# Two LoRA layers in one kernel: features dealt out anew, both weights loaded 32 partitions at a time, and a second product of the weights in seven parts

## The chip, the cores and the metric

The kernel runs on one core of a Trainium2 chip. The core has a matrix engine (TensorE, PE in the profile), three engines for elementwise work (VectorE or DVE, ScalarE or ACT, GpSimd or POOL), a sequencer that does nothing here but issue transfers (SyncE or SP), and 16 DMA engines that carry the transfers. PE reads SBUF and writes PSUM, which has eight banks of 128 x 512 float32. The metric is the device time in microseconds, the median of several runs; lower is better. All data are float32.

## The reference, cut to what matters

```python
# L0: labeler_index has 8 entries here; x is (8, 256, 1024)
base  = einsum('bsi,oi->bso', x, W0)
low   = einsum('bsi,bir->bsr', x, lora_A0[labeler_index])      # rank 32
x = x + base + einsum('bsr,or->bso', low, lora_B0_w) * 0.5
# L1
base  = einsum('bti,oi->bto', x, W1) + b
low   = einsum('bti,bir->btr', x, lora_As1[adapter_mapping])   # rank 16
x = x + base + einsum('btr,bro->bto', low, lora_Bs1[adapter_mapping]) * 2.0
```

W0 and W1 are 1024 x 1024; x has 2048 rows. With the residuals a layer is x(I + W^T) plus a term of low rank. The kernel multiplies the two layers together first, M = (I + W0)^T (I + W1)^T, and then has one large product x M, with the adapters of both layers put into a term of rank 48 and a bias row.

## The kernel before, in words

**M = A B by blocks.** A comes from W0 as loaded (`w0n`, 128 partitions x 8 chunks x 1024), B from W1 transposed (`w1T`, same shape). Both are cut in 2 x 2 blocks of 512. The outer scheme has seven block products instead of eight; P1 = A11 B11 is wanted by itself (`m22` holds it for later), and M11 = A11 B11 + A12 B21. The 512 features between the layers that belong to half i are chunks 4i to 4i+3 of `w0n` and `w1T`: feature 512 i + 4 p + m lies at partition p, chunk 4 i + m.

**The seven groups of products before the main loop**, in PE's order:
- 15 warm-up matmuls on the identity (L918).
- P1: for each of four tiles m of 128 rows and four chunks k, a 128x256 matmul on the first 256 columns (`first`, L949 to L964), then the same on the other 256 (L967 to L970). `keep_p1` has ACT copy each tile's bank to `m22`.
- A12 B21 (`product2`, L308): 16 matmuls of 128x512, added in PSUM on top of P1; ACT copies the sums to `m11`.
- `prepare_down(0)` (L698): 8 matmuls of 128x512, whose stationary operand is `a1`, the eight gathered adapter matrices of layer 1 side by side. It needs all eight.
- `prepare_up` (L668), `finish_up`, `prepare_down(1)`, `prepare_cross`, then the other block products of the weights (`w_groups`, `Chain`), of which the last are themselves split in seven by `product` (L514) with quarters of 128 x 256; `form` (L571) adds seven kept products up to four quarters on DVE.

**Loads.** SP issues everything that comes from DRAM for the weights: `load_w1` (four transfers of 32 partitions for each call, because DVE transposes W1 in blocks of 32 x 32, L225), `load_w0` (one transfer of 128 partitions for each chunk and half of the columns). `load_a1(b)` (L196) is different: ACT reads the index of batch b into a register (L197), issues one transfer of 64 KB from the chosen adapter (L198), and POOL copies it into `a1` (L202). It is called three batches at a time between the tiles of `product2` (L975).

**The identity.** I + W is made in place: a DVE or POOL instruction adds the identity on the diagonal of a chunk (L185 for `w0n`, L233 for `w1T`). DVE does those of the first half; POOL does those of the second half (L233 for h = 1, L982).

**The order.** The instructions of each of the five engines run in the order in which the program names them (`tc.manual_schedule(engines=ORDERED)`, L894). An instruction that waits holds everything behind it on its engine, transfers that the engine issues included. Waits between engines are put in by the compiler from the reads and writes of tiles.

Of the kernel before, what the change touches and what calls it, by code (L numbers as in the profile page):

```python
# [10 lines left out]
ALU = mybir.AluOpType  # L11
# [9 lines left out]
P = 128  # L21
NH = 512
# [5 lines left out]
NWARM = 15  # L28
NV7 = 7
# [5 lines left out]
NQ = NH // 2  # L35
NB = 4
NX = 2
SQ = 32
# [4 lines left out]
def kernel(  # L43
# [11 lines left out]
    lora_b1: bass.AP,  # L55
    out: bass.AP,
):

# [70 lines left out]
    def fix_indices(rawi, n: int, layer: int):  # L131
        wrap = const.tile([1, B], I32, tag=f"wrap{layer}", name=f"wrap{layer}")
        nc.vector.tensor_scalar(wrap, rawi, 0, n, ALU.is_lt, ALU.mult)
        fixed = const.tile([1, B], I32, tag=f"fixed{layer}", name=f"fixed{layer}")
        nc.vector.tensor_tensor(fixed, rawi, wrap, ALU.add)
        nc.vector.tensor_scalar(fixed, fixed, 0, n - 1, ALU.max, ALU.min)
        return fixed

    def index(fixed, b: int, n: int, engine=SP):
        return nc.values_load(  # L140
            fixed[0:1, b : b + 1],
            engines=[engine],
            min_val=0,
            max_val=n - 1,
            skip_runtime_bounds_check_because="clamped on the chip",
        )
# [11 lines left out]
                )  # L158
        return xq

    def new_w1(h: int, i: int):
        both = units[:, 4 * h + 2 * i : 4 * h + 2 * i + 2].rearrange("p u n -> p (u n)")
        return both.rearrange("p (t c) -> p t c", t=NR)

    def load_w1(wq, h: int, i: int, lo: int = 0, hi: int = NR):

        rows = slice(h * NH + lo * SQ, h * NH + hi * SQ)
        for g in range(NG):
            cols = slice(i * NH + g * P, i * NH + (g + 1) * P)
            nc.sync.dma_start(  # L170
                wq[g * SQ : (g + 1) * SQ, lo:hi, :],
                w1[rows, cols].rearrange("(t q) c -> q t c", q=SQ),
            )

    def load_w0(k: int, i: int):
        cols = slice(i * NH, (i + 1) * NH)
        rows = w0[(k // NB) * NH : (k // NB + 1) * NH, cols]
        nc.sync.dma_start(  # L178
            w0n[:, k, cols], rows.rearrange("(p m) c -> p m c", m=NB)[:, k % NB, :]
        )  # L180

    def diag_w0(k: int):
        diag = w0n[:, k].rearrange("p (i q m) -> p i m q", i=2, m=NB)[:, k // NB, k % NB]
        engine = nc.vector if k < NB else nc.gpsimd
        engine.tensor_tensor(diag, diag, ident, ALU.add)  # L185

    def load_b0():
        nc.sync.dma_start(
            b0.rearrange("p (i m) r -> p i (m r)", i=2),
            lora_b0.rearrange("(i p m) r -> p i (m r)", i=2, m=NB),  # L190
        )


    a1_rows = work[:, 0 : 2 * NH].rearrange("p (b k r) -> p b k r", b=B, k=NK)

    def load_a1(b: int):  # L196
        j = index(fixed1, b, N1, mybir.EngineType.Activation)  # L197
        nc.scalar.dma_start(  # L198
            a1_rows[:, b].rearrange("p (i m) r -> p i (m r)", m=NB),
            lora_a1[bass.ds(j, 1)].rearrange("o (i p m) r -> p (o i) (m r)", i=2, m=NB),  # L200
        )
        nc.gpsimd.tensor_copy(a1[:, :, b, :], a1_rows[:, b])  # L202

    def load_down(b: int):
# [15 lines left out]
            )  # L220


    def turn_w1(wq, h: int, k: int, lo: int = 0, hi: int = NR):
        cols = slice(h * NH + lo * SQ, h * NH + hi * SQ)
        nc.vector.transpose(  # L225
            w1T[:, k, cols].rearrange("p (t q) -> p t q", q=SQ),
            wq[:, lo:hi].rearrange("p t (q m) -> p m t q", m=NB)[:, k % NB],
        )
        if k // NB == h:
            part = slice(lo * SQ // NB, hi * SQ // NB)  # L230
            diag = w1T[part, k, cols].rearrange("p (q m) -> p m q", m=NB)[:, k % NB]
            engine = nc.vector if h == 0 else nc.gpsimd
            engine.tensor_tensor(diag, diag, ident[part, part], ALU.add)  # L233

    def turn_x(xq, unit: int):
        xT = units[:, unit].rearrange("p (k t) -> p k t", k=NB)
# [238 lines left out]
    def quarters(x):  # L475
        return x[:, 0:2, 0:P], x[:, 2:4, 0:P], x[:, 0:2, P:T], x[:, 2:4, P:T]

    def z_sums(x, z):
        x11, x12, x21, x22 = x
        nc.vector.tensor_tensor(z[0], x21, x22, ALU.add)  # L480
        nc.vector.tensor_tensor(z[1], z[0], x11, ALU.subtract)
        nc.vector.tensor_tensor(z[2], x11, x21, ALU.subtract)
        nc.vector.tensor_tensor(z[3], x12, z[1], ALU.subtract)


    SLOT = {2: 0, 3: 1, 4: 2, 5: 3, 7: 4, 1: 5, 6: 6}
# [3 lines left out]
    def slot(ps, i: int):  # L490
        n, pos = BANK[i]
        return ps[n][:, pos * NQ : (pos + 1) * NQ]
# [78 lines left out]
    def form(v, ps=None, dst=None):  # L571
# [21 lines left out]
        nc.vector.tensor_tensor(mid, src_two(3, 0), two(1), ALU.add)  # L593
        nc.vector.tensor_tensor(d[:, 3 * NQ : 4 * NQ], src(5), at(6), ALU.add)  # L594

    m12 = {}

    def sums_m(m: int):
# [5 lines left out]
    class Chain:  # L604
# [33 lines left out]
            z_sums(self.q(name), self.z[name])  # L638

        def preload(self):  # L640

            p = m22[:, self.tiles, :].rearrange("p m (h n) -> p (m h) n", h=2)
            for i, part in ((2, 0), (4, 2), (5, 3)):
                nc.scalar.copy(slot(self.X, i), p[:, part])
            nc.vector.tensor_tensor(slot(self.X, 3), p[:, 1], p[:, 3], ALU.subtract)
            for i in (1, 7):
                nc.vector.memset(slot(self.X, i), 0.0)

        def product(self, ps, name, which, first, low=None):
            product(ps, self.q(name), self.z[name], w_ops[which], first, low=low)  # L650
# [17 lines left out]
    def prepare_up():  # L668
        tile = work[:, 4 * NH : 6 * NH]
        part = [tile[:, h * NH : (h + 1) * NH] for h in range(NO)]  # L670
        for h in range(NO):
            cols = slice(h * NH, (h + 1) * NH)
            pm = new_bank()
            for k in range(NK):
                g = k % 4
                nc.tensor.matmul(  # L676
                    pm[g * R0 : (g + 1) * R0, :],
                    b0[:, k, :],
                    w1T[:, k, cols],
                    start=(k < 4),  # L680
                    stop=(k >= NK - 4),
                )
            nc.scalar.copy(part[h], pm)
        return part
# [13 lines left out]
    def prepare_down(h: int):  # L698
        pm = new_bank()
        for k in range(NK):  # L700
            nc.tensor.matmul(  # L701
                pm,
                a1[:, k].rearrange("p b r -> p (b r)"),
                w0n[:, k, h * NH : (h + 1) * NH],
                start=(k == 0),
                stop=(k == NK - 1),
            )
        nc.scalar.copy(gT[h], pm)
# [185 lines left out]
    with tc.manual_schedule(engines=ORDERED):  # L894
        make_identity(nc, ident)
        mid = NR // 2
        wq = {}
        wq[0, 0] = new_w1(0, 0)
        for n in range(2):
            load_w1(wq[0, 0], 0, 0, n * mid, (n + 1) * mid)  # L900
            if n == 0:
                for k in range(NB):
                    load_w0(k, 0)
        wq[0, 1] = new_w1(0, 1)
        load_w1(wq[0, 1], 0, 1)
        for k in range(NB, NK):
            load_w0(k, 0)
        for i in range(2):
            wq[1, i] = new_w1(1, i)
            load_w1(wq[1, i], 1, i)  # L910
        load_b0()
        for k in range(NK):
            load_w0(k, 1)
        nc.scalar.copy(s_all[:, 0:R0], ident[:, 0:R0])

        pw = banks[6][:, 0:P]
        for _ in range(NWARM):
            nc.tensor.matmul(pw, ident, ident, start=True, stop=True)  # L918
        raw0, raw1 = load_indices(idx0, 0), load_indices(idx1, 1)
        nc.gpsimd.memset(scale, L1_SCALING)  # L920
        for half in range(2):
# [27 lines left out]
        def first(g, k: int, n: int):  # L949
            cols = slice(n * NH // 2, (n + 1) * NH // 2)  # L950
            nc.tensor.matmul(  # L951
                g.p1[:, cols],
                g.a[0][:, k, :],
                w1T[:, k, cols],
                start=False,
                stop=(k == NB - 1),
                skip_group_check=True,
            )

        for k in range(NB):  # L960
            turn_w1(wq[0, 0], 0, k, 0, mid)
            diag_w0(k)
            for g in w_groups:
                first(g, k, 0)  # L964
        for k in range(NB):
            turn_w1(wq[0, 0], 0, k, mid, NR)
        for m, g in enumerate(w_groups):  # L967
            for k in range(NB):
                first(g, k, 1)
            g.keep_p1(m22[:, m, :])  # L970
        fixed0, fixed1 = fix_indices(raw0, N0, 0), fix_indices(raw1, N1, 1)
        for k in range(NB, NK):
            turn_w1(wq[0, 1], 0, k)
        for m, g in enumerate(w_groups):
            for b in range(3 * m, min(3 * m + 3, B)):  # L975
                load_a1(b)
            g.product2(m11[:, m, :])
        for k in range(NB):
            turn_w1(wq[1, 0], 1, k)
        for k in range(NB):  # L980
            turn_w1(wq[1, 1], 1, NB + k)
        for k in range(NB, NK):  # L982
            diag_w0(k)
        for k in range(NB):
            sums_w1_first(k)
        prepare_down(0)
        part = prepare_up()
        w_groups[0].sums()
        sums_w1_last()
        finish_up(part)  # L990
        prepare_down(1)
        prepare_cross()
        for which in ("t2", "t1"):
            w_ops[which].sums_dma()
# [286 lines left out]
```

## Time and profile before

| what | value |
|---|---|
| time, median of 3 runs (lowest, highest) | 336.07 us (335.89, 336.35) |
| time of the profiled execution | 336.54 us |
| its span, first to last instruction | 334.8 us |
| PE busy | 329.6 us, 1496 instructions |
| DVE busy | 246.2 us |
| ACT busy | 61.3 us |
| POOL busy | 67.9 us |
| P1's first matmul starts | 7.33 us |
| `product2` (16 matmuls of 128x512) | 22.32 to 36.05 us on the chain that ended last |

A span is the time from the first to the last instruction; the execution is 1.74 us longer than it. In the timeline a row has its start, its length (of several instructions, from the first start to the last end), the engine, the line, the operation, what it writes and reads, and in brackets how long the engine stood idle before it and what ended that. A float32 matmul is recorded as two instructions, so that x32 are 16 matmuls. PE's rows of weights being loaded (PEld) run beside its matmuls.

### The profile page before, as it was taken

How to read it: one execution, taken by the hardware profiler on the slowest of the kernel's cores; microseconds unless marked ns; L12 is line 12 of the kernel's file. 1: busy time of each engine (PE TensorE's matmuls, PEld its weight loads, DVE VectorE, ACT ScalarE, POOL GpSimd, SP SyncE). 2: the span in 40 equal slices, each digit the busy share in tenths (PEclk: the TensorE clock that was granted, in tenths of full speed). 3: DMA queues.
4: the chain of work that ended last, by engine and by line, in shares of the span. 5: the costliest groups of instructions: out<-in, count | busy, mean ns of one | idle time of the engine just before them, and what ended most of it. 6: DMA issues, size and time to landing. Idle time of an engine off the chain costs nothing.

```text
span 334.8 us, 4443 instructions
## 1 busy us (share of the span) xinstructions
PE 329.6 (98%) x1496; PEld 245.1 (73%) x1496; DVE 246.2 (74%) x466; ACT 61.3 (18%) x128; POOL 67.9 (20%) x125
## 2 busy tenths in 40 slices
PE   8999999999999999999999999999999999999996
PEld 8774434544488877888877887877888777788875
DVE  5752697159899999999997856985675986323964
ACT  1022043300034132440001330001331001322000
POOL 7001261540042232771023100012200010000000
PEclk9999999999999999999999999999999999999999
DMA  7949982990062980786277300275500121100113
GB/s 211 199 133 186 271 191 46 168 173 14 0 95 63 194 137 14 113 133 104 95 191 204 79 2 0 74 222 148 116 10 0 63 96 63 64 2 0 63 65 126
DMA packets 66399, 34.53 MB, mean 103 GB/s; under 512 B 47300, under 2 KB 61124, under 8 KB 66376
## 3 DMA queue, kind: packets, MB, share of 16 engines
q1 hardware_dynamic: 56520, 21.13, 27.9%
q0 software_dynamic: 7680, 12.59, 17.4%
q10 hardware_dynamic: 2176, 0.52, 1.0%
q8 instruction: 12, 0.20, 0.2%
q14 instruction: 11, 0.09, 0.1%
HBM read 19.55 MB, written 8.39 MB: 83 GB/s over the span
## 4 chain that ended last, share of the span: by engine, by line
PE 94%; DMA 2%; SPq 1%; DVE 1%; issue 0%; ACT 0%; DVEq 0%
PE bank L523 66%; PE bank L286 14%; PE bank L747 4%; PE bank L701 4%; DMA units<-in_L_cond_W_dram 2%; PE bank L951 2%; PE bank L676 1%; PE bank L765 1%; SPq L170 1%; DVE w1T L225 1%; PE bank L690 1%; SPq L178 1%; DVE w1T L233 0%; PE bank L736 0%; PE bank L715 0%
## 5 line engine op out<-in xcount | busy, mean ns | idle before, releaser
L509 DVE TENSOR_TENSOR work<-bank,work 128x512 f32<-128x512 f32 (+1 forms) x56 | 32.7, 620 | 19.0 <-PE bank L523 18.8
L505 ACT COPY work<-bank 128x512 f32<-128x512 f32 (+1 forms) x56 | 25.8, 548 | 43.0 <-PE bank L523 42.6
L225 DVE STREAM_TRANSPOSE w1T<-units 128x512 f32<-128x512 f32 (+1 forms) x20 | 17.3, 901 | 18.0 <-DMA units<-in_L_cond_W_dram 17.9
L888 POOL DMA_DIRECT2D out_dram<-work x12 | 9.0, 752 | 100.6 <-DVE work L594 100.6
L523 PE MATMUL bank<-w0n,w1T 128*128 128x256 f32 x104 | 24.6, 384 | 0.0
L755 ACT ACTIVATE a<-bank,shift,scale 128x256 f32<-128x256 f32 x8 | 4.5, 564 | 103.3 <-PE bank L747 103.3
L523 PEld LDWEIGHTS bank<-w0n,w1T 128*128 128x128 f32 x104 | 19.3, 190 | 4.1 <-issue 1.7
L523 PE MATMUL bank<-w0n,m 128*128 128x256 f32 x88 | 21.2, 384 | 0.0
L523 PE MATMUL bank<-w1T,s_all 128*128 128x256 f32 x80 | 20.2, 379 | 0.0
L238 DVE STREAM_TRANSPOSE units<-units 128x512 f32<-128x512 f32 x32 | 19.9, 676 | 0.2
L523 PEld LDWEIGHTS bank<-w0n,m 128*128 128x128 f32 x88 | 16.4, 190 | 3.4 <-issue 1.4
L523 PE MATMUL bank<-tw,m 128*128 128x256 f32 x68 | 17.5, 382 | 0.0
L523 PEld LDWEIGHTS bank<-w1T,s_all 128*128 128x128 f32 x80 | 15.2, 190 | 2.1
L523 PE MATMUL bank<-tw,s_all 128*128 128x256 f32 x64 | 16.1, 379 | 0.0
L747 PE MATMUL bank<-units,down 128*64 128x256 f32 x128 | 15.6, 385 | 0.0
L523 PE MATMUL bank<-m,units 128*128 128x256 f32 x64 | 15.1, 379 | 0.0
L951 PE MATMUL bank<-w1T,w0n 128*128 128x256 f32 x64 | 14.5, 383 | 0.5 <-DVE w1T L233 0.5
L523 PEld LDWEIGHTS bank<-tw,m 128*128 128x128 f32 x68 | 12.8, 190 | 2.4 <-issue 0.7
L523 PE MATMUL bank<-w0n,s_all 128*128 128x256 f32 x56 | 14.4, 379 | 0.0
L286 PE MATMUL bank<-tw,s_all 128*128 128x512 f32 x32 | 14.3, 595 | 0.0
L951 PEld LDWEIGHTS bank<-w1T,w0n 128*128 128x128 f32 x64 | 12.3, 196 | 2.4 <-DVE w1T L233 1.3
L701 PE MATMUL bank<-w0n,a 128*128 128x512 f32 x32 | 14.1, 592 | 0.0
(249 smaller groups left out, 646.8 us busy)
## 6 DMA issues: line engine op xcount, KB each, us to landing
units<-in_x_dram SPq DMA_DIRECT2D x128, 64.0 KB, 2.4
out_dram<-work POOLq DMA_DIRECT2D x12, 512.0 KB, 3.5
w0n<-in_L_cond_W_dram SPq DMA_DIRECT2D x16, 256.0 KB, 6.1
units<-in_L_cond_W_dram SPq DMA_DIRECT2D x12, 256.0 KB, 4.9
out_dram<-work SPq DMA_DIRECT2D x3, 512.0 KB, 3.2
units<-in_L_cond_W_dram SPq DMA_DIRECT2D x8, 128.0 KB, 4.6
down<-in_L_cond_lora_A_dram SPq DMA_DIRECT2D x32, 32.0 KB, 2.4
up<-in_L_cond_lora_Bs_dram SPq DMA_DIRECT2D x16, 64.0 KB, 2.7
```

The lines of the kernel that those rows point to most:

```text
L170: nc.sync.dma_start(wq[g * SQ : (g + 1) * SQ, lo:hi, :], w1[rows, cols].rearrange("(t q) c -> q t c", q=SQ),)
L225: nc.vector.transpose(w1T[:, k, cols].rearrange("p (t q) -> p t q", q=SQ), wq[:, lo:hi].rearrange("p t (q m) -> p m t q", m=NB)[:, k % NB],)
L238: nc.vector.transpose(xT[:, NX * j : NX * (j + 1), :].rearrange("p c (t q) -> p c t q", q=SQ), xq[:, :, j, :].rearrange("p t (q c) -> p c ...
L286: nc.tensor.matmul(pm, a[:, k, :], b(k), start=first and k == 0, stop=(k == NB - 1), skip_group_check=not first,)
L505: nc.scalar.copy(at_home(v, n), whole(ps, n))
L509: nc.vector.tensor_tensor(at_home(v, n), whole(ps, n), at_home(v, n), ALU.add)
L523: nc.tensor.matmul(slot(ps, i) if dst is None else dst, lhs, rhs, start=BANK[i][0] not in started, stop=stop, skip_group_check=True,)
L701: nc.tensor.matmul(pm, a1[:, k].rearrange("p b r -> p (b r)"), w0n[:, k, h * NH : (h + 1) * NH], start=(k == 0), stop=(k == NK - 1),)
L747: nc.tensor.matmul(pl[half * MLOW : (half + 1) * MLOW, :], down[:, half * NB + k, :], x_b[half][:, k, :], start=(k == 0), stop=(k == NB - ...
L755: nc.scalar.activation(lows[:, b % NLOW], pl, mybir.ActivationFunctionType.Identity, bias=shift[:, 0:1], scale=scale[:, 0:1],)
L888: eng.dma_start(out[b, :, h * NH : (h + 1) * NH].rearrange("(j p) d -> p j d", p=P), ob[:, 0:D].rearrange("p (j d) -> p j d", d=NH),)
L951: nc.tensor.matmul(g.p1[:, cols], g.a[0][:, k, :], w1T[:, k, cols], start=False, stop=(k == NB - 1), skip_group_check=True,)
```

## The change

- **Features dealt out anew.** Feature 256 g + 128 i + 4 q + m now lies at partition 32 g + q, chunk 4 i + m. Each group of 32 partitions holds 256 neighbouring features.
- **Loads.** `load_w0` issues four transfers of 32 partitions for a call, with several chunks in each. `load_w1` can load one half of the features or both: the second half of W1's rows now comes with both at once, in rows of 1 KB where they were of 512 B. `load_b0` is two transfers in place of one. `load_a1` is two transfers for each batch, one issued by ACT as before and one issued by POOL, each with its own index register; POOL's copy follows as before. The four loads of batches 0 to 3 and 4 to 7 stand after tiles 1 and 3 of P1.
- **Identity.** With the new order the diagonal lies in other columns and all of its additions are DVE's: on 32 or 64 partitions, by chunk (`add_identity_to`) or for four chunks at once (`add_identity`).
- **A12 B21.** `Second` makes it in inner form: for each pair of tiles seven products of quarters, two 128x256 matmuls each. P1's quarters are loaded into the banks first (`load_inner`: three ACT copies; `load_inner_3`: one DVE subtraction; `zero_inner`: two memsets), sums of the operands are made on DVE (`z_sums`, `Operand.sums`), ACT keeps the seven products (`keep`) and DVE forms the quarters of `m11` (`form`).
- **Order.** `prepare_down(1)` follows `prepare_down(0)`; the transposes of W1's second half, all remaining identities and W0's second half of columns come after the `Second` products in the program.
- The warm-up matmuls write to four banks in turn.

```diff
+    def load_w1(h: int, lo: int, hi: int, first: int = 0, last: int = 2):
         rows = slice(h * NH + lo * SQ, h * NH + hi * SQ)
         for g in range(NG):
+            cols = slice((2 * g + first) * P, (2 * g + last) * P)
             nc.sync.dma_start(
+                wq[h][g * SQ : (g + 1) * SQ, lo:hi, first * P : last * P],
                 w1[rows, cols].rearrange("(t q) c -> q t c", q=SQ),
             )
+    def load_w0(i: int, h: int, lo: int = 0, hi: int = NB):
+        rows = w0.rearrange("(g i q m) c -> g i q m c", g=NG, i=2, m=NB)
+        cols = slice(h * NH, (h + 1) * NH)
+        for g in range(NG):
+            nc.sync.dma_start(
+                w0n[g * SQ : (g + 1) * SQ, NB * i + lo : NB * i + hi, cols],
+                rows[g, i, :, lo:hi, cols],
+            )
...
     def load_a1(b: int):
-        j = index(fixed1, b, N1, mybir.EngineType.Activation)
-        nc.scalar.dma_start(
-            a1_rows[:, b].rearrange("p (i m) r -> p i (m r)", m=NB),
-            lora_a1[bass.ds(j, 1)].rearrange("o (i p m) r -> p (o i) (m r)", i=2, m=NB),
-        )
+        for i, engine in enumerate((nc.scalar, nc.gpsimd)):
+            j = index(fixed1, b, N1, engine.engine)
+            rows = lora_a1[bass.ds(j, 1)].rearrange("o (g i q m) r -> i g (o q) (m r)", g=NG, i=2, m=NB)
+            engine.dma_start(
+                a1_rows[:, b, NB * i : NB * (i + 1)].rearrange("p m r -> p (m r)"),
+                rows[i],
+            )
         nc.gpsimd.tensor_copy(a1[:, :, b, :], a1_rows[:, b])
...
+    class Second:
+        op = Operand(
+            lambda j, n: w1T[:, NB + 2 * j : NB + 2 * j + 2, n * NQ : (n + 1) * NQ],
+            s_all[:, 0 : 4 * 2 * NQ].rearrange("p (i c n) -> p i c n", i=4, c=2),
+        )
+        def __init__(self, n: int):
+            self.tiles = slice(2 * n, 2 * n + 2)
+            self.ps = sets[1 - n]
...
+        def products(self, plan):
+            product(self.ps, self.x, self.z, self.op, "loaded", plan=plan)
+        def form(self):
+            form(self.kept, dst=m11[:, self.tiles, :].rearrange("p m n -> p (m n)"))
+    def load_inner(ps, tiles):
+        p = m22[:, tiles, :].rearrange("p m (h n) -> p (m h) n", h=2)
+        for i, part in ((2, 0), (4, 2), (5, 3)):
+            nc.scalar.copy(slot(ps, i), p[:, part])
...
         for k in range(NB):
+            turn_w1(0, k, 0, mid)
+            add_identity_to(w1T, k, 0, 1)
+            add_identity_to(w0n, k, 0, 2)
             for g in w_groups:
                 first(g, k, 0)
+        fixed0, fixed1 = fix_indices(raw0, N0, 0), fix_indices(raw1, N1, 1)
+        seconds = [Second(n) for n in range(2)]
+        zero_inner(seconds[0].ps)
         for k in range(NB):
+            turn_w1(0, k, mid, NR)
+            add_identity_to(w1T, k, 1, 2)
         for m, g in enumerate(w_groups):
             for k in range(NB):
                 first(g, k, 1)
             g.keep_p1(m22[:, m, :])
+            if m % 2:
+                load_inner(seconds[m // 2].ps, seconds[m // 2].tiles)
+                for b in range(4 * (m // 2), 4 * (m // 2) + 4):
+                    load_a1(b)
+        one, other = seconds
         for k in range(NB, NK):
-            turn_w1(wq[0, 1], 0, k)
-        for m, g in enumerate(w_groups):
-            for b in range(3 * m, min(3 * m + 3, B)):
-                load_a1(b)
-            g.product2(m11[:, m, :])
...
+            turn_w1(0, k)
+        add_identity(w1T, 1, 0, 2)
+        add_identity(w0n, 1, 0, 2)
+        zero_inner(other.ps)
+        one.products([1, 2])
+        other.products([1, 2])
+        z_sums(one.x, one.z, 0, 2)
+        Second.op.sums()
+        z_sums(one.x, one.z, 2, 4)
+        load_inner_3(one.ps, one.tiles)
+        one.products([6, 5, 4, 7, 3])
+        keep(one.kept, one.ps)
+        load_inner_3(other.ps, other.tiles)
+        z_sums(other.x, other.z)
+        for i in range(2):
+            load_w0(i, 1)
+        other.products([6, 5, 4, 7, 3])
+        keep(other.kept, other.ps)
+        prepare_down(0)
+        for n in range(2):
+            for k in range(NK):
+                turn_w1(1, k, n * mid, (n + 1) * mid)
+        for i in range(2):
+            add_identity(w1T, i, 2, 4)
+        for k in range(NK):
+            add_identity_to(w0n, k, 2, 4)
+        prepare_down(1)
+        part = prepare_up()
         for k in range(NB):
             sums_w1_first(k)
-        prepare_down(0)
-        part = prepare_up()
         w_groups[0].sums()
+        for second in seconds:
+            second.form()
         sums_w1_last()
         finish_up(part)
-        prepare_down(1)
         prepare_cross()
```

## The prediction

> **What bounds the kernel now.** I read the page first, then the chain that ended last in order of time, then POOL's and ACT's timelines, then single lines.
>
> ```profile
> span 334.8 us, 4443 instructions
> PE 329.6 (98%) x1496; PEld 245.1 (73%) x1496; DVE 246.2 (74%) x466; ACT 61.3 (18%) x128; POOL 67.9 (20%) x125
> ```
>
> PE is the bound, and it hardly waits. The chain shows the stage that the change touches:
>
> ```profile
> 16.43 5.89 PE bank L951 x26
> 22.32 13.73 PE bank L286 x32
> 36.05 6.87 PE bank L701 x16
> ```
>
> These are start, length and line. P1 ends at 22.3 us, A12 B21 (L286) runs without a gap to 36.05, and `prepare_down(0)` (L701) follows without a gap, so its stationary operand `a1` was ready. From 36.05 to the end PE runs on with no wait to speak of: 334.8 - 36.05 = 298.75 us of work. Whatever moves the start of L701 therefore moves the end. `a1` comes from POOL's copies:
>
> ```profile
> 24.94 0.29 POOL L202 COPY a<-work 128x128 f32<-128x128 f32 x1 [16.29 <-DMA work<-in_L_cond_lora_As_dram]
> 25.96 0.29 POOL L202 COPY a<-work 128x128 f32<-128x128 f32 x1 [0.73 <-DMA work<-in_L_cond_lora_As_dram]
> 28.95 0.29 POOL L202 COPY a<-work 128x128 f32<-128x128 f32 x1 [2.70 <-DMA work<-in_L_cond_lora_As_dram]
> 31.89 0.65 POOL L202 COPY a<-work 128x128 f32<-128x128 f32 x2 [2.65 <-DMA work<-in_L_cond_lora_As_dram]
> 33.89 1.01 POOL L202 COPY a<-work 128x128 f32<-128x128 f32 x3 [1.36 <-DMA work<-in_L_cond_lora_As_dram]
> ```
>
> The eight copies end at 34.9 us, 1.15 us ahead of L701. POOL only waits for transfers here; ACT issues them, several in flight. The cover is thin.
>
> **What a POOL instruction behind a waiting one does.** The same timeline, later:
>
> ```profile
> 62.15 2.77 POOL L433 DMA_DIRECT2D units<-w1T  x2
> 68.07 0.90 POOL L433 DMA_DIRECT2D units<-units  x1 [3.15 <-DMA units<-w1T]
> 68.64 0.62 POOL L784 COPY down<-g 128x128 f32<-128x128 f32 x1
> ```
>
> The third transfer of a set waits 3.15 us for the first to land, and the copies of L784, whose operands ACT had finished by 61.7 (L737 at 61.09, 0.58 long), start only after it. POOL runs strictly in order, and a wait for its own transfer stops it.
>
> **The change, part by part.**
>
> *The gathered adapters, the step that decides.* `load_a1(b)` now has POOL read an index, issue half of batch b, and copy batch b. The copy waits for that half to land, and the index read and transfer of b + 1 stand behind the copy. Eight round trips run one after another where eight transfers overlapped. The prices:
>
> ```profile
> L198 ACTq DMA_DIRECT2D work<-in_L_cond_lora_As_dram x8: 387/392/444, 23.0 to 30.8; - x8
> ...
> DMA to landing us min/median/max: 1.9/4.9/5.5
> ```
>
> (ns and times of the ACT issue of 64 KB; us to landing.) POOL's own transfers landed after 3.5 us (L128, two of 32 bytes) and 3.3/4.5/6.5 us (L433, 256 KB, min/median/max). SP's 32 KB adapters (L207) had a median of 2.4 us.
> - First copy. Tile 1's `keep_p1` copy ends at 18.91 + 0.59 = 19.5 in the trace; three preload copies follow (L644, 0.38 us each): 20.65. ACT's first issue came 0.11 us after its copy before (22.94 to 23.05), so 20.8. Landing takes 1.9 to 5.5 us; I take 1.9, which the first of these loads had. Copy 0.29: batch 0 done at 23.0. POOL's half of batch 0 is issued long before.
> - One round trip. Index read: three ACT issues took 2.33 us, (2.33 - 0.39) / 2 = 0.97 apart, less the issue's own 0.39 leaves 0.58. It may run beside the copy (0.29), so only the longer counts. Landing: at least 2.4, at most 6.5; the nearest row on this queue is 3.5. A step is 2.4 + 0.29 = 2.7 at least, 6.5 + 0.58 + 0.29 = 7.4 at most; I take 3.5 + 0.58 = 4.1.
> - Contention. DMA is full from 26 to 46 us (share 1.19 and 1.13 in two ten-microsecond windows, then 0.38). ACT's loads took a median of 3.0 us over their least; for half the bytes I add 1.5 us to the three steps before about 43 us (0 to 3.0 each).
> - Sum: 23.0 + 3 x 5.6 + 4 x 4.1 = 56.2 us. L701 moves by 56.2 - 36.05 = +20.15 us. At 2.7 a step it would be 41.9 (+5.8); at 7.4, with the first landing at 5.5, 26.6 + 51.8 = 78.4 (+42.3).
>
> The Trainium skill, "DMA: Bandwidth & Descriptors", section "Anatomy of one DMA — SWDGE (gpsimd) path", puts one such transfer at about 2.0 us plus bytes / 436,000, an estimate of 2.1 us for 32 KB. With it the step would be 2.7 and the wait the lower one above; of the rows above, POOL's queue has none that short, its least being 3.3.
>
> *A12 B21 in seven parts.* Sixteen matmuls of 128x512 took 13.73 us, 0.86 each. Fourteen of 128x256 for each of two pairs are 28; four such of L523 took 93.52 - 91.79 = 1.73 us, 0.43 each: 12.04 us, **-1.7**. Ahead of them DVE must transpose four chunks (18.29 + 4.07 = 22.4), add two identities (0.38 each by L185) and two memsets (0.55): 23.7, so PE waits 1.4 us after P1 and ends at 35.7, not 36.05. DVE's further sums (8 of 0.42, 4 of 0.69, 2 of 0.43) stay ahead: the last that `one` needs is done by 28.6, when PE comes to it at 30.5. Net gain 0.3 us, at most 1.7; all of it is covered by the wait for `a1`, so I count 0.
>
> *Loads.* Four more W0 transfers stand before W1's second quarter, 4 x 0.47 = 1.9 us of SP's time; DMA share is 1.2 from 8 to 16 us, so bytes and not issues set that arrival. 0 to +1.9 us on P1 and the first copy; taken 0. Wider W1 rows can only bring the second half earlier, which nothing on the path then wants. One more b0 transfer: 0.4 us on SP, hidden.
>
> *Identities on DVE, `form`, order.* Ten `form` additions (6 of 0.42, 4 of 0.69: 5.3 us) and the identities POOL had (8) fall in the time when PE waits for `a1` or does the 19.8 us of preparation (36.05 to 55.85). Without that wait the second half's transposes would be late: 8 of 0.64 from its arrival at 38.65 end at 43.8, with identities 44.9, against 42.6 for `prepare_down(1)`. That is the second rival.
>
> *PE after the wait.* PE has no idle time over 1 us in the trace after its start. At the start it is slow: the 15 warm-ups took 6.11 us, 0.41 each, where 128 columns should take half of 0.43. That is 2.9 us lost, though the granted clock in that row reads 1.00. After some 20 us of rest it may lose nothing or 2.9 again; the start is the nearest row: **+2.9**.
>
> The Trainium skill, "TensorE: Matmul & The Clock Gate", Part 1, says that an idle window of about 3.4 us halves the clock and a busy one restores it, an estimate of 1.7 us lost; that would take 1.2 us off the sum.
>
> **Sum.** 336.54 (profiled execution) + 20.15 + 2.9 = 359.6; less 0.47, by which that execution is above the median, **359.1 us**.
>
> **Rivals.**
> - *The seven parts pay* (faster). If each step of the adapter chain took under (34.0 - 23.0) / 7 = 1.6 us, `a1` would be there when the products end, and with DVE's 1.4 us hidden by an earlier arrival of W1 the time would be 336.07 - 1.7 = 334.4. For it: PE's count is lower. Against: no load of adapters in the trace landed in under 1.9. Chance 0.05. With the 1.4 us paid it is 335.8, no change: 0.02.
> - *DVE becomes the bound before `prepare_down(1)`* (338.1): same condition on `a1`, and 44.9 - 42.6 = 2.3 us of wait less the 0.3 gained. It decides once a step of the chain is under 1.6 us and the second half arrives no earlier than now. Chance 0.05.
> - *The chain holds, but short* (342 to 348): steps near 2.7 and no slow restart, 336.07 + 5.8 = 341.9. For it: SP's 32 KB landings. This is inside the forecast's case.
>
> **How the numbers follow.** The adapter chain sets the end: 0.88, with its own range from the bounds. The range 344 to 371 leaves out the rivals (0.12) and about a tenth of the main case: 344 is steps of 3.0 with no slow restart (23.0 + 21.0 = 44.0, +8.0), 371 is a wait of 32 us and 2.9, all steps 6.4. Smaller than 0.2% (0.67 us) can't be told from no change. Faster 0.05, same 0.02, slower 0.93 (0.88 and 0.05).
>
> **What the profile of after would show.** Right: POOL's timeline alternates one transfer, an idle of 2 to 5 us ended by a DMA, and one copy, eight times; PE has one gap of some 20 us ending when the last copy of `a` ends; L701 starts at 45 to 68 us; the matmuls after the gap are slower for some us; from there the rest takes about 298.75 us. Wrong: several POOL transfers of adapters in flight at once, copies done by 36 us, or PE's longest gap ended by DVE or by W0's second half.

## The result, and the profile after

The changed kernel takes 366.31 us (median of 4 runs, 365.72 to 366.54) where the kernel before took 336.03 beside it: 1.0897 of it, 95% interval 1.0878 to 1.0916. The forecast was 359.1, within 344 to 371.

The page of the profile after: span, busy times, and of the 40 slices PE's share and the clock granted to it, in tenths.

```profile
span 364.6 us, 4608 instructions
PE 332.7 (91%) x1520; PEld 252.4 (69%) x1520; DVE 260.3 (71%) x514; ACT 64.1 (18%) x138; POOL 68.9 (19%) x125
PE   7944804999999999999999999999999999999996
PEclk9995955999999999999999999999999999999999
```

PE has little more work than before (332.7 us, 329.6 before) in a span 29.8 us longer. Nearly all of the loss lies in the first seven slices of 9.1 us, and in three of these, the fourth, the sixth and the seventh, PE was granted only some half of its clock. PE's timeline there (start, length, line, and in brackets the idle time before and what ended it):

```profile
32.36 5.84 PE L546 MATMUL bank<-w1T,w0n 128*128 128x256 f32 x16 [9.80 <-DMA w0n<-in_L_cond_W_dram]
42.36 1.89 PE L546 MATMUL bank<-s_all 128*128 128x256 f32 x8
59.50 2.05 PE L546 MATMUL bank<-s_all,w0n 128*128 128x256 f32 x4 [15.25 <-DMA units<-in_x_dram]
61.34 1.92 PE L546 MATMUL bank<-s_all 128*128 128x256 f32 x4
63.04 1.52 PE L546 MATMUL bank<-w1T,s_all 128*128 128x256 f32 x4
65.37 14.00 PE L759 MATMUL bank<-w0n,a 128*128 128x512 f32 x32 [0.81 <-POOL a L226]
```

`prepare_down(0)` (L759) starts at 65.37 instead of 36.05, 29.3 us later, and from there to the end are 299.2 us, where before had 298.75. But PE does not wait once: it has three gaps, 9.80 + 15.25 + 0.81 = 25.9 us. After each of the two long ones it is slow for a while: the 8 matmuls (x16) take 5.84 us, and the last 6 take 5.06 (59.50 to 64.56), where run 9 below, without such gaps, has 3.62 and 2.76.

POOL's timeline from the fifth adapter on (L222 issues, L226 copies):

```profile
36.30 0.66 POOL L222 DMA_DIRECT2D work<-in_L_cond_lora_As_dram  x1 [0.99 <-DMA units<-in_L_cond_W_dram]
42.32 0.29 POOL L226 COPY a<-work 128x128 f32<-128x128 f32 x1 [5.36 <-DMA work<-in_L_cond_lora_As_dram]
43.28 0.66 POOL L222 DMA_DIRECT2D work<-in_L_cond_lora_As_dram  x1 [0.67 <-issue]
53.09 0.29 POOL L226 COPY a<-work 128x128 f32<-128x128 f32 x1 [9.15 <-DMA work<-in_L_cond_lora_As_dram]
54.04 0.66 POOL L222 DMA_DIRECT2D work<-in_L_cond_lora_As_dram  x1 [0.66 <-issue]
60.66 0.29 POOL L226 COPY a<-work 128x128 f32<-128x128 f32 x1 [5.96 <-DMA work<-in_L_cond_lora_As_dram]
61.61 0.66 POOL L222 DMA_DIRECT2D work<-in_L_cond_lora_As_dram  x1 [0.66 <-issue]
64.66 0.66 POOL L226 COPY a<-work 128x128 f32<-128x128 f32 x1 [2.38 <-DMA work<-in_L_cond_lora_As_dram]
```

One issue, one wait, one copy, as forecast; the eight copies start at 23.10, 26.64, 30.57, 34.97, 42.32, 53.09, 60.66 and 64.66 us. The last ends at 65.32, and L759 follows 0.05 us later. The steps are 3.5 to 4.4 us long up to 35 us, then 7.4, 10.8 and 7.6, and 4.0 at the end.

W0 comes more slowly than before. Four rows of the table by stretches; the last two columns are the busy share of the DMA engines and GB/s. The first is of before while the second half of W0's columns loads, the others are of after:

```profile
38.00:44.00 6.00, 6.00 (x24) 2.32 (x26) 5.26 (x6) 0.59 (x1) 2.73 (x5) 1.00 1.06 366
```
```profile
48.00:52.00 4.00, 0.00 (x0) 0.00 (x0) 3.70 (x8) 0.00 (x0) 0.00 (x0) 0.50 1.08 195
52.00:56.00 4.00, 0.00 (x0) 0.00 (x0) 0.00 (x0) 0.00 (x0) 0.96 (x2) 0.50 1.10 203
60.00:64.00 4.00, 4.00 (x11) 3.14 (x10) 0.00 (x0) 0.00 (x0) 0.95 (x2) 0.50 0.56 129
```

The engines are full in the first three and carry 366 GB/s in transfers of 128 partitions, some 200 in transfers of 32. In the column ahead of them stands the granted clock: 1.00 in the first row, where PE works, 0.50 in the next two, where it waits, and still 0.50 in the last, where it works again. That is why the matmuls behind the wait are slow.

The theory to test was that POOL's chain alone set the end (**theory 1**). The 15.25 us gap spoke for a rival: that the second pair's products waited for the W0 loads that stand just ahead of them in the program (**theory 2**), two waits that end within a microsecond of each other. The row names an x load as what ended the wait, but the trace also keeps the semaphores, the counters to which transfers report that they have landed and on which instructions wait. PE waited here for those of the last four W0 loads, issued from 45.33 to 50.17; the last of these landed at 59.41, and PE went on at 59.47. The x loads behind them use the same semaphores again. So the second wait is one for W0; what it costs the runs have to show.

### The profile page after: what moved, and what is told of

The parts are those of the page before. It is cut to its first block, busy times and chain, and to the rows that moved or that the text cites. A ratio compares the mean times of both kernels' runs of the same rounds, so it can differ in the third digit from the quotient of the medians.

```text
span 364.6 us, 4608 instructions
## 1 busy us (share of the span) xinstructions
PE 332.7 (91%) x1520; PEld 252.4 (69%) x1520; DVE 260.3 (71%) x514; ACT 64.1 (18%) x138; POOL 68.9 (19%) x125
## 4 chain that ended last, share of the span: by engine, by line
PE 80%; issue 7%; DMA 3%; ACT 2%; SPq 2%; ACTq 2%; DVE 1%; POOL 1%; POOLq 0%; DVEq 0%
PE bank L546 61%; PE bank L305 8%; PE bank L805 4%; PE bank L759 4%; DMA units<-in_L_cond_W_dram 2%; DMA work<-in_L_cond_lora_As_dram 1%; ACTq L222 1%; PE bank L734 1%; PE bank L823 1%; SPq L182 1%; ACT units L450 1%; SPq L172 1%; POOL work L222 1%; DVE w1T L249 1%; PE bank L1009 1%
## 5 line engine op out<-in xcount | busy, mean ns | idle before, releaser
L249 DVE STREAM_TRANSPOSE w1T<-units 128x256 f32<-128x256 f32 (+1 forms) x28 | 17.6, 675 | 9.8 <-DMA units<-in_L_cond_W_dram 9.7
L546 PE MATMUL bank<-w1T,s_all 128*128 128x256 f32 x88 | 22.8, 386 | 0.0
L546 PEld LDWEIGHTS bank<-w1T,s_all 128*128 128x128 f32 x88 | 17.2, 196 | 2.5
L546 PE MATMUL bank<-s_all,w0n 128*128 128x256 f32 x8 | 3.1, 523 | 15.3 <-DMA units<-in_x_dram 15.3
L1009 PE MATMUL bank<-w1T,w0n 128*128 128x256 f32 x64 | 14.3, 382 | 1.0 <-DVE w0n L206 0.8
L546 PE MATMUL bank<-w1T,w0n 128*128 128x256 f32 x16 | 5.8, 544 | 9.8 <-DMA w0n<-in_L_cond_W_dram 9.8
L759 PE MATMUL bank<-w0n,a 128*128 128x512 f32 x32 | 14.0, 595 | 0.8 <-POOL a L226 0.8
```

Source lines behind the costliest of these rows:

```text
L249: nc.vector.transpose(w1T[:, k, cols].rearrange("p (t q) -> p t q", q=SQ), wq[h][:, lo:hi].rearrange("p t (i q m) -> p i m t q", i=2, m=NB ...
L546: nc.tensor.matmul(slot(ps, i) if dst is None else dst, lhs, rhs, start=BANK[i][0] not in started, stop=stop, skip_group_check=True,)
L759: nc.tensor.matmul(pm, a1[:, k].rearrange("p b r -> p (b r)"), w0n[:, k, h * NH : (h + 1) * NH], start=(k == 0), stop=(k == NK - 1),)
L1009: nc.tensor.matmul(g.p1[:, cols], g.a[0][:, k, :], w1T[:, k, cols], start=False, stop=(k == NB - 1), skip_group_check=True,)
```

## The experiments

**1. POOL issues all eight transfers, then copies.** The chain goes, the rest stays.

```diff
     def load_a1(b: int):
...
-        nc.gpsimd.tensor_copy(a1[:, :, b, :], a1_rows[:, b])
...
+        for b in range(B):
+            nc.gpsimd.tensor_copy(a1[:, :, b, :], a1_rows[:, b])
```

> All eight of POOL's adapter transfers are issued before the first copy; nothing else differs from the changed kernel. Theory 1 (the chain of POOL's round trips alone moves the end): the last copy comes at some 34 to 42 us in place of 65.3, and the time falls by 20 to 29 us, to 337 to 346. Theory 2 (two waits of PE end within 1 us of each other: without the chain the products of A12 B21 would still end at 64.6, since a product waits for the second half of W0's columns): the copies come as early, but the time falls only by 0 to 4 us, to 362 to 366.

364.0 us (363.65 to 364.25), 1.0821 [1.0792, 1.085] of before: 2.3 us gained of 30. POOL's last copy, and PE's third row of products:

```profile
39.48 0.29 POOL L1038 COPY a<-work 128x128 f32<-128x128 f32 x1 [2.69 <-DMA work<-in_L_cond_lora_As_dram]
58.54 2.04 PE L545 MATMUL bank<-s_all,w0n 128*128 128x256 f32 x4 [13.31 <-DMA units<-in_x_dram]
63.03 13.90 PE L758 MATMUL bank<-w0n,a 128*128 128x512 f32 x32
```

`a1` is ready at 39.8, 25.5 us earlier, and the products still stand still until 58.5. There is a second wait of the same length.

**2. W0's second half of columns behind the second pair's products.** Theory 2's wait goes, the chain stays.

```diff
         z_sums(other.x, other.z)
-        for i in range(2):
-            load_w0(i, 1)
         other.products([6, 5, 4, 7, 3])
         keep(other.kept, other.ps)
+        for i in range(2):
+            load_w0(i, 1)
```

> The loads of W0's second half of columns stand behind the second pair's products in the program; POOL's chain is as in the changed kernel. Theory 1 and theory 2: PE's gap of 15.25 us inside the products goes and the products end at about 45, but the last adapter copy still comes at 58 to 66, so the time stays at 360 to 367. Theory 3 (the wait inside the products alone sets the end): 345 to 352.

368.11 us (366.96 to 368.76), 1.0936 [1.0899, 1.0974], just above the expected 360 to 367.

```profile
43.75 1.03 PE L546 MATMUL bank<-s_all,w0n 128*128 128x256 f32 x4
45.47 1.03 PE L546 MATMUL bank<-w1T,s_all 128*128 128x256 f32 x4
64.50 16.82 PE L759 MATMUL bank<-w0n,a 128*128 128x512 f32 x32 [18.00 <-POOL a L226]
```

The products now run through and end at 46.5: the 15.25 us were the wait for W0. PE stands 18 us for POOL's chain instead, and the chain gives the same end by itself. The 16 matmuls behind that rest take 16.82 us where run 1 took 13.90: **2.9 us** of slow restart.

**3. Both.**

> Both edits. Theory 2: PE does prepare_down(0) from about 45 to 52 and then waits for W0's second half and its identities, which come at about 60; the time falls by 10 to 14 us, to 352 to 356. Theory 1: the same time as with POOL's copies alone taken out of the chain.

353.17 us (352.07 to 353.43), 1.0501 [1.0474, 1.0529]. Only now does the time fall by much, 13.1 us below the changed kernel, where the two edits alone gave -2.3 and +1.8. `prepare_down(0)` starts at 46.27.

**4. Both, and both adapter halves issued by POOL, none by ACT.**

```diff
-        for i, engine in enumerate((nc.scalar, nc.gpsimd)):
-            j = index(fixed1, b, N1, engine.engine)
+        j = index(fixed1, b, N1, nc.gpsimd.engine)
+        for i, engine in enumerate((nc.gpsimd, nc.gpsimd)):
```

> Both edits, and both halves of the adapters are issued by POOL, none by ACT. Theory 2 with the first gap (9.8 us before the products) laid to SP's transfers standing behind ACT's: that gap shrinks below 2 us, ACT copies the banks of tiles 2 and 3 without its wait of 6 us, and the time falls by 20 to 28 us, to 338 to 346. If the first gap is due to the transfers of 32 partitions being slow in themselves, it stays above 6 us and the time is that of both edits, 350 to 356.

347.81 us (347.69 to 348.24), 1.0338 [1.0311, 1.0365], above the expected 338 to 346. PE's first gap and SP's issues of the quarter of W0 that it waits for, in run 3 and then in run 4:

```profile
32.13 5.67 PE L545 MATMUL bank<-w1T,w0n 128*128 128x256 f32 x16 [9.48 <-DMA w0n<-in_L_cond_W_dram]
14.37 14.50 SPq L182 DMA_DIRECT2D w0n<-in_L_cond_W_dram  x4
```
```profile
27.05 6.25 PE L545 MATMUL bank<-w1T,w0n 128*128 128x256 f32 x16 [4.66 <-DMA w0n<-in_L_cond_W_dram]
11.23 3.22 SPq L182 DMA_DIRECT2D w0n<-in_L_cond_W_dram  x4
```

Once ACT issues no adapters, SP's four issues take 3.2 us instead of 14.5, and the gap is halved. So SP's loads were held up by ACT's adapter transfers; the changed kernel's table of waits has the same pair, 9.5 us the longest:

```profile
SPq L182 <- DMA work<-in_L_cond_lora_As_dram: 12.3, 3, 9.5
```

The link is in the semaphores that the trace keeps. SP's and ACT's transfers take turns on the same eight, and an issue waits until the transfer that had its semaphore before has landed. In the changed kernel SP's second, third and fourth load of that quarter wait on the semaphores of ACT's second, third and fourth adapter: these landed at 24.61, 26.64 and 28.54, and SP issued at 24.62, 26.66 and 28.55. In run 4 the four loads wait on none of the adapters' semaphores. What was missed in the expectation: the 4.66 us of the gap that stay (the DMA engines are full there, share 1.18 from 24 to 26 us), 2.6 of slow matmuls after it, and 5.9 later on (waits for W0's second half, and 2.68 for ACT's copy of the cross term).

**5. W0 again by one transfer of 128 partitions for each chunk, in the new order of features.**

```diff
-        rows = w0.rearrange("(g i q m) c -> g i q m c", g=NG, i=2, m=NB)
+        rows = w0.rearrange("(g i q m) c -> i m g q c", g=NG, i=2, m=NB)
...
+        for m in range(lo, hi):
+            nc.sync.dma_start(w0n[:, NB * i + m, cols], rows[i, m, :, :, cols])
```

> Only load_w0 differs from the changed kernel: one transfer of 128 partitions for each chunk, as before the change, with the features in the new order. If the transfers of 32 partitions are what slows the loads, W0's second half lands in 4 to 7 us (some 350 GB/s, as before) in place of 9 and more, the adapters' late landings of 6 to 10 us shrink to 3 to 5, the last copy comes at 50 to 56 and the time is 350 to 357. If it is the number of bytes in flight, the landings and the time stay within 3 us of the changed kernel. The product that waited for all of W0's second half may also wait no longer; by theory 2 the adapter chain then sets the end alone.

385.19 us (384.41 to 385.51), 1.1449 [1.1426, 1.1473]: far worse, against both theories. The same table by stretches, and PE:

```profile
26.00:30.00 4.00, 4.00 (x20) 3.63 (x20) 3.96 (x5) 1.64 (x5) 0.00 (x0) 1.00 0.27 103
49.72 1.03 PE L543 MATMUL bank<-s_all,w0n 128*128 128x256 f32 x4
81.23 16.68 PE L756 MATMUL bank<-w0n,a 128*128 128x512 f32 x32 [28.76 <-POOL a L223]
```

With the source split in 4 groups of 32 rows the DMA engines are busy to 0.27 and carry 103 GB/s, as if four of sixteen worked. The Trainium skill, "DMA: Bandwidth & Descriptors", section "Why a DMA increments its semaphore by 16 and not by 1", says that the number of engines is the largest up to 16 that divides the outermost dimension of both sides; 4 groups give 4 engines, which the 0.27 agrees with. One thing of value: here the second pair's products run through (49.72, no bracket), though the loads of W0's second half stand ahead of them as in the changed kernel, and SP issues them only from 51.55 on. So the wait of 15.25 us goes with the shape of the transfers. The product reads only W0's first 512 columns, which had long landed; four chunks in one transfer span an address range that covers them, one chunk's does not. That the compiler put in the wait for this reason is argued from this run, not tried by itself.

**6. Runs 1, 4 and 5 together.**

> W0 by 128 partitions a transfer, both halves of the adapters issued by POOL, all copies behind all issues; the place of W0's second half in the program is that of the changed kernel. If the shape of the transfers is the rest of the loss: both waits of PE (4.7 us before the products, 2 us and more before prepare_down(1)) go below 1.5 us each, and the time is 337 to 342. If not, 346 to 350, as with W0 by 32 partitions.

371.34 us (369.6 to 372.82), 1.1055 [1.1013, 1.1097]. Both expectations, written before run 5's cause was read, miss it: W0 still comes on a quarter of the engines, and the first gap is 16.77 us.

**7. The adapters by 32 partitions, on top of run 2.** Do the adapters land late because their own transfers, too, have only 4 groups outermost?

```diff
-        for i, engine in enumerate((nc.scalar, nc.gpsimd)):
+        for engine, groups in ((nc.scalar, (0, 1)), (nc.gpsimd, (2, 3))):
...
+            for g in groups:
+                engine.dma_start(
+                    a1_rows[g * SQ : (g + 1) * SQ, b].rearrange("p (i m) r -> p i (m r)", m=NB),
+                    rows[g],
+                )
```

> Against the kernel with W0's second half behind the products (368.1 us), where the chain of adapters alone sets the end: each half batch is now two transfers of 32 partitions (ACT groups 0 and 1, POOL groups 2 and 3), whose outermost dimension in DRAM is 32 rows, in place of one of 128 partitions whose outermost dimension in DRAM is four groups. POOL still copies batch by batch. If a transfer with four outermost groups runs on four of the 16 DMA engines and queues there, the landings of 6 to 10 us shrink to 3 to 5 in spite of the second issue (0.7 us), the last copy comes at 52 to 58 and the time is 354 to 362. If the landings are long because of the bytes in flight alone, the last copy comes at 64 to 70 and the time is 368 to 374.

369.62 us (369.36 to 370.41), 1.1007 [1.0991, 1.1023]. The landing that took 9.8 us in the changed kernel takes 9.6 (42.49 to 52.08). The next took 5.4 where run 2 had 7.3, but the first steps took longer, and the last copy ends later than there (66.28 against 64.45). The shape of the adapters' transfers is not what makes that landing long.

**8. A12 B21 in seven parts alone, in the kernel before.** The features and the shapes of all transfers are as before. The adapters are issued earlier, one after each tile of P1 and then the rest, the loads of W0's second half stand behind the first pair's products, and the warm-up matmuls are those of the changed kernel.

```diff
-        for m, g in enumerate(w_groups):
...
-            g.product2(m11[:, m, :])
+        one.products([1, 2])
+        other.products([1, 2])
...
+        other.products([6, 5, 4, 7, 3])
+        keep(other.kept, other.ps)
```

> The kernel before, features and load shapes as they were, with A12 B21 in seven parts alone (P1 preloaded, kept in units, formed on DVE after the transposes of W1's third quarter and after the first sums of W1), adapters loaded whole by ACT one batch after each tile of P1, the rest after. If the seven parts are worth what their matmuls say (28 of 0.43 for 16 of 0.86) and the adapters come in time, 334.0 to 335.0, faster than both kernels. If the adapters or the sums on DVE make PE wait, 336 to 339.

336.57 us (12 runs, 335.99 to 337.59), 1.0011 [0.9997, 1.0026]: nothing gained that can be told. PE starts right after P1, but:

```profile
22.34 3.96 PE L527 MATMUL bank<-w1T,w0n 128*128 128x256 f32 x16
27.01 1.99 PE L527 MATMUL bank<-s_all 128*128 128x256 f32 x8 [0.71 <-DVE s_all L423]
29.32 1.14 PE L527 MATMUL bank<-s_all,w0n 128*128 128x256 f32 x4 [0.32 <-DVE bank L633]
36.34 7.03 PE L740 MATMUL bank<-w0n,a 128*128 128x512 f32 x16
```

PE waits 0.71 + 0.32 us for DVE, whose memsets (L637) had waited 1.11 and 0.34 us for ACT's preload copies, which stood behind adapter issues.

**9. The same in another order:** transposes and memsets ahead of the preload copies, the adapters' issues behind them.

```diff
+            if m == 3:
+                for k in range(NB, NK):
+                    turn_w1(wq[0, 1], 0, k)
+                zero_inner(other.ps)
             if m % 2:
                 load_inner(seconds[m // 2].ps, seconds[m // 2].tiles)
+            load_a1(m)
...
+        one.form()
         for k in range(NB):
             turn_w1(wq[1, 0], 1, k)
-        one.form()
...
-        other.form()
         w_groups[0].sums()
+        other.form()
```

> The kernel before's loads and adapters with A12 B21 in seven parts, as in the run before it (336.57 us, 1.0011), in another order of DVE's and ACT's work: the transposes of W1's second quarter and the two memsets of the second pair's banks stand ahead of that pair's preload copies, the adapters' other issues behind them, one.form() ahead of the second half's transposes, other.form() behind the first sums of the next stage. All of the computation is there. Theory 'the seven parts lost their gain to DVE': the 0.71 + 0.32 us in which PE waited for L423 and L633 go, the last quarter's transposes end by 43.2 instead of 45.1, the products end by 35.3 instead of 36.3, prepare_down(0) starts there, and the time is 334.4 to 335.6 us, 0.995 to 0.999 of the kernel before. Theory 'the gain isn't there to have' (the adapters' later issues, or forms that delay the sums behind them, give back what the order gains): PE waits 0.5 us or more for the last copies of a, or for the sums of the next stage ahead of product6, and the time stays at 336.0 to 337.

**334.04 us** (333.96 to 334.72), 0.9945 [0.9929, 0.9961] of before: faster than both kernels.

```profile
21.24 3.62 PE L527 MATMUL bank<-w1T,w0n 128*128 128x256 f32 x16
24.69 1.89 PE L527 MATMUL bank<-s_all 128*128 128x256 f32 x8
33.32 7.03 PE L740 MATMUL bank<-w0n,a 128*128 128x512 f32 x16
```

That is also below the expected 334.4 to 335.6. No bracket is left. The products take 33.32 - 21.24 = 12.08 us where before took 13.73, 1.65 us less; the medians differ by 1.9 us and the profiled spans by 2.6 (332.2, 334.8). In this profiled execution P1 also ended 1.1 us earlier; what of that is the edit is not known.

**10. Run 2 with W0's second half held back until `prepare_down(0)` is done,** by two ACT copies into its place. Are the long landings the W0 bytes in flight?

```diff
         prepare_down(0)
+        for i in range(2):
+            nc.scalar.copy(w0n[:, NB * i : NB * (i + 1), NH : NH + 1], gT[0][:, 0:NB].unsqueeze(2))
+        for i in range(2):
+            load_w0(i, 1)
```

> As the run with W0's second half behind the products, but two small ACT copies after prepare_down(0) write to the place where that half goes, so that its 2 MB cannot be in flight while the adapters' chain runs. Theory 'the long landings are the W0 bytes in flight': POOL's copies up to about 42 us stay as they were, the landing that took 9.6 us (42.4 to 52.0) and the one of 7.3 take 2.5 to 4.5, the last copy ends at 52 to 58 us and prepare_down(0) starts there. W0's second half then comes late and the time says little: 350 to 370 us. Theory 'the landings are long for another reason (the queue itself, or the reads of the adapters)': they stay at 6 to 10 us, the last copy ends at 62 to 66, prepare_down(0) starts there, and the time is 372 to 385.

371.54 us (one run), above the expected 350 to 370. POOL's last copies, PE, and the stretch from 48 to 52 us:

```profile
43.45 0.66 POOL L222 DMA_DIRECT2D work<-in_L_cond_lora_As_dram  x1 [0.67 <-issue]
48.18 0.29 POOL L226 COPY a<-work 128x128 f32<-128x128 f32 x1 [4.06 <-DMA work<-in_L_cond_lora_As_dram]
51.73 0.38 POOL L226 COPY a<-work 128x128 f32<-128x128 f32 x1 [1.94 <-DMA work<-in_L_cond_lora_As_dram]
55.09 0.29 POOL L226 COPY a<-work 128x128 f32<-128x128 f32 x1 [1.76 <-DMA work<-in_L_cond_lora_As_dram]
55.44 9.23 PE L759 MATMUL bank<-w0n,a 128*128 128x512 f32 x16 [9.13 <-POOL a L226]
73.42 8.77 PE L759 MATMUL bank<-w0n,a 128*128 128x512 f32 x16 [8.76 <-DVE w0n L206]
48.00:52.00 4.00, 0.00 (x0) 0.00 (x0) 3.97 (x8) 0.18 (x1) 1.23 (x3) 0.68 0.06 9
```

With the DMA engines idle (0.06) a step takes 3.4 to 3.6 us, and the chain ends at 55.4 instead of 65.3. Its first half, beside W1's loads, is as it was (42.49). So the landing of 9.8 us was long because W0's second half was in flight ahead of it. The x loads, which stand behind W0 on SP, are held back here too, so that a part of the step of 7.6 us may have been theirs: in the changed kernel they are issued from 51.36 on. The time is no better since W0's second half then comes late.

## Why the prediction was right, and where it was not

**Right: POOL's chain, its place and its form.** Eight serial round trips, L759 behind the last copy (0.05 us), inside 45 to 68 us, and the rest of the kernel unchanged (299.2 against 298.75). Run 2 shows that the chain alone gives this end.

**Mis-sized: the contention term.** The sum put 1.5 us of it on the three steps before 43 us and none behind. Those early steps were shorter than the 5.6 I took (3.5, 3.9 and 4.4); the later ones, for which I took 4.1, were 7.4, 10.8 and 7.6. The steps add up to 41.6 us from the first copy against 33.2 forecast, and the chain ended at 65.3 instead of 56.2, +9.1. I had taken from the trace of before that DMA is full only up to 46 us, and had set the loads of the change at 0. But SP issues W0's second half from 41.98 on, where before did from 34.30, and in transfers of 32 partitions it runs at some 200 GB/s instead of 366, so that it is in flight until 59.4 us. The trace of before had a hint of that rate: from 26 to 32 us, while W1 came in transfers of 32 partitions (rows of 512 B), full engines (share 1.14) carried 199 GB/s. Run 10, with that half held back, has steps that add up to 32.0 us.

**Counted, but hidden here: the slow restart of 2.9 us.** In the changed kernel L759 took 14.00 us: PE had worked since 59.50, and the last six matmuls took the loss, 5.06 us where run 9 took 2.76 (30.73 to 33.49), covered by the chain. Where PE does rest until L759, run 2 pays 2.9. The Trainium skill, "TensorE: Matmul & The Clock Gate", Part 1, was read as 1.7: after 18.0 us of rest it was 2.9, after 9.13 and 8.76 (run 10) 2.2 and 1.7 (9.23 and 8.77 against 7.03). The granted clock of 0.50 in these waits agrees with its rule. In run 3, though, a wait of 1.93 us inside L758 was followed by a clock of 0.50 too (the 8 matmuls behind it took 8.80 us, the 8 ahead of it 7.03), which an idle window of 3.4 us does not account for.

Together: +9.1 - 2.9, +0.5 in the rest, and 0.47 that the profiled execution of before was above the median make the 7.2 us between 359.1 and 366.3.

**Wrong: one gap of some 20 us ended by the last copy.** It is the point that I had named as a sign against me: PE's longest gap was ended by W0's second half. "Products end 35.7" failed twice: the first products waited 9.80 us for W0's second quarter (SP held up by ACT's adapter transfers), and the second pair's 15.25 for columns that it does not read. The list of the change has W0's second half of columns behind the `Second` products; its loads stand ahead of the second pair's last five, as the diff shows. I had costed four more issues on SP, but not that a load moved ahead of a product in the program can become that product's wait. It was luck that this cost the forecast nothing: the wait ended 0.8 us before the chain did (64.56 and 65.32). Run 1 takes 2.3 us off, run 2 adds 1.8, both take 13.1 off. With a chain as short as forecast (56.2), this wait would have set the end by itself, near the 364.0 us of run 1, and the sum had no term for it.

**The price of a POOL transfer by the Trainium skill** ("DMA: Bandwidth & Descriptors", section "Anatomy of one DMA — SWDGE (gpsimd) path", an estimate of 2.1 us) comes near where nothing else is in flight: from the start of the issue to the copy run 10 has 2.6 and 2.4 us. It was 9.8 beside W0.

**The -1.7 of the seven parts** is there, but not for nothing: with DVE and ACT in the first order it is lost (run 8), in the second it is found (run 9).

**The rivals.** Neither faster case nor "DVE becomes the bound" could show: their condition, steps under 1.6 us, was never met; the shortest step in any run with the chain was 3.4 (run 10, with the engines idle).

**What stays open:** why 32-partition transfers of 2 KB rows carry some half of what 128-partition ones do (in run 10, with nothing else in flight, W0's second half ran at 218 GB/s with the engines full, 68 to 70 us); by what rule a transfer of several pieces holds up an instruction that reads none of them; and when a short wait halves the clock.

## What to carry to other kernels

On an engine that runs in order, a transfer and the copy that waits for it make a chain of full round trips once the next transfer is issued behind the copy: issue them all first. Price such a chain by what will be in flight in the changed kernel, not in the one before, and when one long wait is found, look for a second that ends just behind it; taking either away alone shows nothing. A transfer that spans several strided pieces can make an instruction wait that reads none of them.

## What the runs showed of the hardware beyond that

- Transfers with 4 groups outermost: DMA share 0.27, 103 GB/s (run 5, 26 to 30 us). Transfers of 32 partitions: share 1.08, 195 GB/s (the changed kernel, 48 to 52 us). Of 128 partitions: 1.06, 366 GB/s (before, 38 to 44 us).
- A 32 KB transfer issued by POOL landed after 2.4 to 2.6 us with the DMA engines idle (run 10), and after 9.8 behind W0's transfers (the changed kernel).
- The granted clock fell to 0.50 in waits of 8.8 us and longer, and 8 to 16 matmuls of 128x512 behind such waits cost 1.7 to 2.9 us more (runs 2 and 10). Shorter waits were followed by 0.50 as well: one of 4.66 us in run 4, and ones of 1.93 us in run 3 and 1.96 us in run 6; another of 1.93 us, in run 4, was not.
